# A graph layer on one core: PSUM banks and loads of the lead-in changed, a fourth bank for slot products

## The chip, the cores and the metric

The kernel runs on one core of a Trainium2 chip. The time is device microseconds of one launch. Where one profiled execution is read, its span is the time between the first and the last recorded instruction.

## The reference

A graph of 6250 nodes (128 features each, float32) and 100000 edges, sorted by their destination. Every edge has one of two types, and each type its own weight and bias; each node sums the messages that come to it, adds its own product, and is normalized:

```python
m_data = X[src] @ W_data.T + b_data
m_ctrl = X[src] @ W_control.T + b_control
msg = where((edge_type == 0)[:, None], m_data, m_ctrl)
agg = segment_sum(msg, dst, num_segments=6250)
out = relu(agg + (X @ W_self.T + b_self))
x = layernorm(x + out)          # over the 128 features
```

## The kernel before

**Products.** The messages are made per node, not per edge: 6250 x 2 types. In the lead-in, 25 steps (`q`) of two blocks of 128 nodes each form `x @ [W_data, W_control]` in a PSUM bank of 512 columns (the bias matmul is L499, the two products L502). The result is kept as three bf16 parts in `m3`: ScalarE copies the bank (part 1, L507), TensorE subtracts that part in the bank through a matmul with minus the identity (L510), a copy by ScalarE or VectorE takes part 2 (`evict`, L444 or L445), and VectorE subtracts part 2 from the bank into part 3 (L514). Every second step the parts go to a DRAM `table` (L518). The `x` pieces come by SyncE's queue (L479): the first ones at once, each later one once the copy of part 1 seven steps before it is done.

**Sums.** The destinations are cut into 39 windows of 160 nodes. A window's sum is a product of a selection matrix with the messages in `m3`. It goes in 25 slot products: stage 1 (L956, four matmuls of 384 columns) gathers source rows for 128 slots into a PSUM bank `g`; ScalarE or VectorE copies it to `gs` (L444, L445); stage 2 (L970, four matmuls of 384 columns, and L973, three of 128) adds the slots to their destinations in an accumulating bank `a`. One slot product is therefore eleven matmuls of 8 x 384 + 3 x 128 = 3456 columns. A closing part adds the nodes' own products (L527, L530, L561) and normalizes.

**Ranks.** What a slot gathers is worked out on the chip, for groups of windows (of 1, 2, and nine times 4; the groups begin at windows 0, 1, 3, 7, 11, 15, 19, 23, 27, 31 and 35). The edges of a group are turned into one-hot rows `hots` (four pieces, one buffer each). Counts (TensorE, L713) go through `csb` to DRAM as `past` (SyncE, L720) and come back into the last four rows of `hots` (SyncE, L724, four loads). Then 22 rank rounds (L738 on TensorE, L744 on VectorE, one PSUM bank `rk`) find each edge's slot; a scatter (L775) places them in `vt`; a copy `vs` goes to DRAM as `packed` (SyncE, L795). From `packed`, each window loads `rows`, 784 KB broadcast over the partitions (SyncE, L927, a ring of three buffers, so that a window's load waits for stage 1 of the window three before it), and VectorE makes the selection from them (L935).

**The order** on every engine is fixed by a planner when the kernel is built. Each operation is added with its engine, a duration from a formula (`act(cols)`, `dve(cols)` or a constant) and a due time; buffers are rings of a given number. The planner simulates these and writes the instructions in the order that comes out. On the chip, each engine runs its row in that order, and SyncE issues its loads and stores in that order too. So a changed duration or number of buffers changes the order everywhere.

**PSUM** has eight banks: `vt` 1, `rk` 1, `ga` 1, `a` 2, `g` 3. Bank `ga` serves group 0's ranks and, much later, the "gathered part" (L1050, L1057), which does the last ten nodes (6250 - 39 x 160) through an indirect load.

Of the kernel before, what the change touches and what calls it, by code (L numbers as in the profile page):

```python
# [10 lines left out]
F32 = mybir.dt.float32  # L11
# [6 lines left out]
ACT = mybir.EngineType.Activation  # L18
# [3 lines left out]
P = 128  # L22
D = 128
# [21 lines left out]
NW = sum(GROUPS)  # L45
# [3 lines left out]
NS = 25  # L49
# [5 lines left out]
GT = [slots_of(16 * min(GN, N - NW * WN - GN * i)) for i in range(NGB)]  # L55
# [187 lines left out]
def dve(cols, rate=1.04):  # L243
    return 0.07 + cols * rate / 1000


def act(cols):
    return 0.055 + cols / 1200

def sums_over_windows(ctx, tc, x, xt, edges, w, bias, out, total):  # L250
    nc = tc.nc
    V, A, G, T, S = nc.vector, nc.scalar, nc.gpsimd, nc.tensor, nc.sync
# [19 lines left out]
    T0 = 36.0  # L272
    TW = 13.0
    LAT = 0.1
    G0, G1 = 0.0, -4
    GC = 1.3
    SPD = 0.45
    RP, RA, RS = 1, 14, 0.9
# [5 lines left out]
        lat=4.0)  # L284
    w_sb = C([D, D3], F32, "w_sb")
# [72 lines left out]
    minus = C([P, P], BF16, "minus")  # L358
# [4 lines left out]
    one3 = C([P, P], BF16, "one3")  # L363
# [17 lines left out]
    def count_rows():  # L381
        for h in range(RH):
# [28 lines left out]
                                    start=True, stop=True), 0.8, [first_f, ident], [first_ps])  # L411
# [22 lines left out]
    brows = C([P, D3], BF16, "brows")  # L434
# [18 lines left out]
    m3 = C([P, NT, D3], BF16, "m3")  # L453
# [3 lines left out]
    past_b = Buf(plan, None, None, None, "past_b")  # L457
    m3_key = lambda g: [(m3, (min(g, NS - 1), i)) for i in range(3)]
    MS = 1.3
    LATE = [12.0, 14.0, 20.0]  # L460
    XB = [12, 12, 12, 13]
    xts = []
# [10 lines left out]
                pieces[q0 + k - i] = (c, k, (xts[c], i))  # L473
            loads[q0 // 2] = (c, i, j, q0)

    def load_x(q, after):
        if q in loads:
            c, i, j, q0 = loads[q]
            add("SP", SPD, lambda: S.dma_start(  # L479
                xf(c)[:, i * P : j * P], xt[:, q0 * P : (q0 + j - i) * P]),  # L480
                4.0 + MS * q - 9, after, [(xts[c], i)], lat=3.0)
    AHEAD = 7
    for q in range(AHEAD):
        load_x(q, [])
    for q in range(NS):
        bs = range(2 * q, min(2 * q + 2, NB))
        nb = len(bs)
        due = 4.0 + MS * q
        mp = B(ps, [P, 512], F32, *(("a", 2) if q % 5 > 2 else ("g", 3)))

        n = 2 * nb * D
        ts = slice(4 * q, 4 * q + 2 * nb)

        for i, b in enumerate(bs):
            c, k, xk = pieces[b]

            def product(i=i, c=c, k=k, mp=mp, nb=nb):
                if i == 0:
                    T.matmul(mp.t[:, : 2 * nb * D].rearrange("p (b f) -> p b f", b=nb), one3.t,  # L499
                             brows.t[:, None, : 2 * D].to_broadcast([P, nb, 2 * D]), start=True,  # L500
                             stop=False, skip_group_check=True)
                T.matmul(mp.t[:, 256 * i : 256 * i + 256], xf(c)[:, k * P : k * P + P],  # L502
                         w_sb.t[:, : 2 * D], start=False, stop=False, skip_group_check=True)
            add("PE", 0.5 if i else 0.71, product, due + 0.5 * i, [xk, w_sb, one3, brows], [mp])
        pv3 = lambda mp=mp, nb=nb: mp.t[:, : 2 * nb * D].rearrange("p (t f) -> p t f", f=D)
        mv3 = lambda i, ts=ts: m3.t[:, ts, i * D : (i + 1) * D]
        add("ACT", act(n), lambda pv3=pv3, mv3=mv3: A.copy(mv3(0), pv3()), due + 0.6, [mp],  # L507
            [(m3, (q, 0))])
        load_x(q + AHEAD, [(m3, (q, 0))])
        add("PE", 0.11 * nb, lambda mp=mp, mv3=mv3, nb=nb: T.matmul(  # L510
            mp.t[:, : 2 * nb * D], minus.t, mv3(0), start=False, stop=True,
            skip_group_check=True), due + 1.2, [minus, (m3, (q, 0))], [mp])
        evict(lambda mv3=mv3: mv3(1), pv3, n, due + 1.8, [mp], [(m3, (q, 1))])
        add("DVE", dve(n), lambda pv3=pv3, mv3=mv3: V.tensor_sub(mv3(2), pv3(), mv3(1)),  # L514
            due + 2.4, [mp, (m3, (q, 1))], [(m3, (q, 2))])
# [114 lines left out]
    def ranks(gi, w0, nw, when, step, engines):  # L630
# [6 lines left out]
        n = nw * KT  # L637
# [43 lines left out]
        else:  # L681
# [235 lines left out]
    def sums(gi, w0, nw, placed):  # L917
# [5 lines left out]
        for i in range(nw):  # L923
# [68 lines left out]
    def gathered(bis, when, step):  # L992
# [37 lines left out]
        for j, bi in enumerate(bis):  # L1030
# [51 lines left out]
    for gi, w0, nw, *_ in todo:  # L1082
# [167 lines left out]
```

## Time and profile before

| | |
|---|---|
| runs | 641.18, 645.41, 647.32 us (median 645.41) |
| the profiled execution | 644.74 us, its span 642.9 us |
| granted TensorE clock, mean | 0.967 |
| TensorE busy | 555.6 us, 86% of the span |
| VectorE busy | 496.3 us, 77% |
| ScalarE busy | 487.6 us, 76% |
| GpSimd busy | 31.3 us, 5% |
| copies `gs` on ScalarE | 927, 391.8 us in sum |
| chain that ended last | TensorE 68%, ScalarE 12%, VectorE 7%, DMA 5% |

Windows are named by their number; 975 slot products (39 x 25) make most of the time. A row of a timeline gives the start, the length, the engine, the line and the tiles of a run of equal instructions, and in brackets how long the engine stood idle before it and what ended that. Line numbers here are those of the kernel before; the changed kernel's are 5 to 11 higher.

### The profile page before, as it was taken

Reading aid. Unit: us, or ns where it says so; the run is one execution under the profiler, and the core shown is the slowest. Engines: PE = TensorE matmul, PEld = TensorE weight load, DVE = VectorE, ACT = ScalarE, POOL = GpSimd, SP = SyncE. Lnnn points to the kernel's source line nnn. Section 1 sums busy time; section 2 is a strip of 40 time slices with the busy share of each in tenths; the row PEclk is TensorE's granted clock in tenths of the full one; section 3 lists DMA queues with packets and bytes.
Section 4 is the critical chain, followed back from the end, with each engine's and each line's share of the span. In section 5 each row is a group of like instructions: output and inputs, shape, how many; then the busy total and the mean of one; then the engine's idle time right before and its main releaser. Section 6 shows DMA issues by size and latency. Waiting matters only on the chain.

```text
span 642.9 us, 32170 instructions
## 1 busy us (share of the span) xinstructions
PE 555.6 (86%) x13810; PEld 427.6 (67%) x13810; DVE 496.3 (77%) x1502; ACT 487.6 (76%) x1258; POOL 31.3 (5%) x32
## 2 busy tenths in 40 slices
PE   5878789459989989898998899889889988989992
PEld 3544567338868777776787687678768767766771
DVE  6679688948988898788699979879987988685411
ACT  3545678348879787787888788888889788778992
POOL 1000100100010001001000100100010010010000
PEclk9989899759999999999999999999999999999997
DMA  3895821162045105403520630351253054022300
GB/s 109 244 303 160 246 58 50 22 188 80 3 125 153 44 33 181 107 6 125 135 63 29 188 106 4 125 165 32 73 147 94 5 185 104 17 90 95 82 16 15
DMA packets 56060, 64.33 MB, mean 100 GB/s; under 512 B 18159, under 2 KB 47828, under 8 KB 55908
## 3 DMA queue, kind: packets, MB, share of 16 engines
q1 hardware_dynamic: 54417, 59.68, 31.0%
q0 software_dynamic: 1120, 2.23, 1.6%
q8 instruction: 110, 1.80, 1.2%
q14 instruction: 43, 0.34, 0.2%
q10 hardware_dynamic: 370, 0.26, 0.2%
HBM read 45.94 MB, written 14.30 MB: 94 GB/s over the span
## 4 chain that ended last, share of the span: by engine, by line
PE 68%; ACT 12%; DVE 7%; DMA 5%; issue 5%; SPq 1%; another core or an unknown queue 0%; ACTq 0%; POOLq 0%; DVEq 0%
PE a L970 24%; PE g L956 23%; ACT gs L444 7%; PE rk L738 5%; PE a L973 5%; PE vt L775 3%; ACT to_d L451 3%; DMA hots<-past 2%; PE rk L713 1%; DVE slot L744 1%; PE g L502 1%; PE a L527 1%; DMA rows<-packed 1%; DVE rows L935 1%; PE vt L862 1%
## 5 line engine op out<-in xcount | busy, mean ns | idle before, releaser
L444 ACT CAST gs<-g 128x384 bf16<-128x384 f32 x927 | 391.8, 483 | 85.4 <-PE g L956 69.1
L956 PE MATMUL g<-m,rows 128*32 128x384 bf16 x3822 | 364.1, 331 | 14.0 <-DVE rows L935 8.4
L970 PE MATMUL a<-gs,hot 128*32 128x384 bf16 x3744 | 341.8, 333 | 34.1 <-ACT gs L444 21.0
L956 PEld LDWEIGHTS <-rows 128*32 128x32 bf16 x3822 | 250.4, 134 | 26.5 <-DVE rows L935 9.5
L970 PEld LDWEIGHTS <-hot 128*32 128x32 bf16 x3900 | 172.7, 95 | 103.7 <-issue 61.9
L973 PE MATMUL a<-gs,hot 128*32 128x128 bf16 x2808 | 231.9, 220 | 0.3 <-issue 0.3
L744 DVE TENSOR_REDUCE slot<-rk 124x4 f32<-124x392 f32 x209 | 117.4, 562 | 49.3 <-PE rk L738 42.8
L973 PEld LDWEIGHTS <-hot 128*32 128x32 bf16 x2925 | 116.7, 97 | 8.4 <-issue 4.6
L943 DVE TENSOR_TENSOR hot<-iota_b,to_d 128x1280 bf16<-128x1280 bf16 (+1 forms) x117 | 95.7, 841 | 0.0
L738 PE MATMUL rk<-hots,tri 128*32 128x392 bf16 (+1 forms) x880 | 86.1, 324 | 9.5 <-DMA hots<-past 5.3
L702 DVE TENSOR_TENSOR hots<-iota_b,st 124x784 bf16<-124x784 bf16 (+2 forms) x120 | 58.6, 506 | 4.9 <-PE vt L775 4.9
L935 DVE TENSOR_SCALAR rows<-rows,pid 128x1568 bf16<-128x1568 bf16 x78 | 46.9, 622 | 16.2 <-DMA rows<-packed 16.1
L738 PEld LDWEIGHTS <-tri 128*32 128x32 bf16 x968 | 38.4, 96 | 18.6 <-issue 13.5
L884 POOL DMA_INDIRECT sr<-table,at x20 | 25.9, 1293 | 476.4 <-DVE to_d L877 425.6
L570 DVE TENSOR_REDUCE s<-a 128x128 f32<-128x384 f32 x39 | 21.7, 556 | 34.6 <-PE a L973 22.9
L775 PEld LDWEIGHTS <-two 124*64 124x64 bf16 x858 | 21.7, 110 | 12.2 <-DVE two L766 5.9
L775 PE MATMUL vt<-hots,two 124*64 124x98 bf16 x836 | 26.1, 210 | 3.4 <-DVE two L766 1.7
L451 ACT COPY to_d<-vs 32x100 bf16<-32x100 bf16 (+3 forms) x84 | 22.2, 265 | 1.3
L760 DVE TENSOR_TENSOR hr<-slot_f,slot 124x768 bf16<-124x768 bf16 (+2 forms) x39 | 20.2, 517 | 2.6 <-ACT slot L448 2.6
L444 ACT CAST gl<-g 64x384 bf16<-64x384 f32 x39 | 18.4, 472 | 4.7 <-PE g L956 4.7
L713 PE MATMUL rk<-hots,later 124*32 124x392 bf16 (+1 forms) x210 | 20.8, 335 | 0.8 <-DVE slot L744 0.8
L766 DVE TENSOR_TENSOR two<-hr,lo 124x768 bf16<-124x768 bf16 (+2 forms) x39 | 20.2, 517 | 0.1
(188 smaller groups left out, 502.1 us busy)
## 6 DMA issues: line engine op xcount, KB each, us to landing
rows<-packed SPq DMA_DIRECT2D x39, 784.0 KB
table<-m SPq DMA_DIRECT2D x12, 768.0 KB
xc<-in_xt SPq DMA_DIRECT2D x9, 320.0 KB
rows<-in_xt SPq DMA_DIRECT2D x8, 256.0 KB
xr<-in_x SPq DMA_DIRECT2D x8, 256.0 KB
out<-xr SPq DMA_DIRECT2D x8, 256.0 KB
gl<-sr SPq DMA_DIRECT2D x39, 48.0 KB
win<-in_edges SPq DMA_DIRECT2D x38, 32.0 KB
```

Source lines behind the costliest of these rows:

```text
L444: [("ACT", act(cols), lambda: A.copy(o(), src())), ("DVE", dve(cols), lambda: V.tensor_copy(o(), src()))], None, None, due, r, w, lat)
L451: "ACT", 0.1 + cols / 1000, lambda: A.copy(o(), src()), due, r, w)
L702: lambda k=k, kn=kn, ci=ci, hs4=hs4: V.tensor_tensor(hv(ci)[:EP, k - KS[ci] : k - KS[ci] + kn].rearrange("p k w (c d) -> p (k w) c d", d=2 ...
L713: T.matmul(cnt.t[R * j : R * j + R, :wide], later.t[:EP, R - 1 - k : 2 * R - 1 - k], flat(k, EP), start=k < 4, stop=k + 4 > KT - 2, skip_g ...
L738: T.matmul(acc.t[R * j : R * j + R, (k - k0) * wide : (k - k0 + 1) * wide], tri.t[:, R * j : R * j + R], flat(k, P), start=k == k0, stop=True,
L744: vec(due, (k1 - k0) * wide, lambda k0=k0, k1=k1, acc=acc: V.tensor_reduce(slot.t[:, k0:k1, :], acc.t[:EP, : (k1 - k0) * wide].rearrange(" ...
L775: T.matmul(vv()[q : q + 64, i // 2, :], two.t[:EP, (k - k0) * nw + i].rearrange("p f r -> p (f r)"), one(k)[:EP, i, :], start=k == 0 and i ...
L935: add("DVE", dve(half * NT, 0.335), lambda sp=sp, rs=rs: V.tensor_scalar(sp.t[:, rs], sp.t[:, rs], pid1.t, None, op0=ALU.is_equal), due - ...
L943: lambda i=i, hot2=hot2, s4=s4, c0=c0, c1=c1: V.tensor_tensor(hot2.t[:, c0:c1].rearrange("p g (c d) -> p g c d", d=2), iota1_b.t.rearrange ...
L956: T.matmul(gp.t[R * t : R * t + R, :D3], sp.t[:, :, 4 * g + t], m3.t[:, 4 * g + t, :], start=True, stop=True)
L970: T.matmul(a.t[R * j : R * j + R, :D3], hot2.t[:, g, R * j : R * j + R], gs.t, start=g == 0, stop=False, skip_group_check=True)
L973: T.matmul(a.t[R * c : R * c + R, D3:], hot2.t[:, g, P:], gs.t[:, c * D : (c + 1) * D], start=False, stop=last, skip_group_check=True)
```

## The change

- `act(cols)`, the planner's duration for a ScalarE copy, is 0.12 + 0.00085 per column instead of 0.055 + 1/1200; the durations of the lead-in's matmuls are lower too.
- The ring of `g` has four banks instead of three, and the bank `ga` is gone: group 0's ranks share `rk` with the others, and the gathered part uses an `a` bank, at the time of window 20.
- The lead-in's message products use the four `g` and two `a` banks (six); before, three `g` and two `a`.
- All `x` pieces are asked for at the start; before, the later ones waited for a part 1 each.
- Part 2 is always copied by ScalarE. In even steps, part 3 is made by a second minus-identity matmul and a copy, by ScalarE or VectorE, instead of VectorE's subtraction.

The diff, with what only renames left out:

```diff
 def act(cols):
-    return 0.055 + cols / 1200
+    return 0.12 + cols * 0.00085
...
-    G0, G1 = 0.0, -4
+    G0 = 20
...
     MS = 1.3
+    LOP = 2
...
-    def load_x(q, after):
+    def load_x(q):
...
-                4.0 + MS * q - 9, after, [(xts[c], i)], lat=3.0)
-    AHEAD = 7
-    for q in range(AHEAD):
-        load_x(q, [])
+                -9.0 + 0.5 * q, [], [(xts[c], i)], lat=3.0 + 0.6 * q)
+    for q in range(NS):
+        load_x(q)
...
-        mp = B(ps, [P, 512], F32, *(("a", 2) if q % 5 > 2 else ("g", 3)))
+        if q % 6 < 4:
+            mp, half = B(ps, [P, 512], F32, "g", 4), 0
+        else:
+            mp, half = B(ps, [P, 512], F32, "a", 2), 0
...
-            add("PE", 0.5 if i else 0.71, product, due + 0.5 * i, [xk, w_sb, one3, brows], [mp])
+            add("PE", 0.43 if i else 0.64, product, due + 0.5 * i, [xk, w_sb, one3, brows], [key])
...
-        load_x(q + AHEAD, [(m3, (q, 0))])
...
-        evict(lambda mv3=mv3: mv3(1), pv3, n, due + 1.8, [mp], [(m3, (q, 1))])
-        add("DVE", dve(n), lambda pv3=pv3, mv3=mv3: V.tensor_sub(mv3(2), pv3(), mv3(1)),
-            due + 2.4, [mp, (m3, (q, 1))], [(m3, (q, 2))])
+        add("ACT", act(n), lambda pv3=pv3, mv3=mv3: A.copy(mv3(1), pv3()), due + 1.8, [key],
+            [(m3, (q, 1))])
+        if q % LOP:
+            add("DVE", dve(n), lambda pv3=pv3, mv3=mv3: V.tensor_sub(mv3(2), pv3(), mv3(1)),
+                due + 2.4, [key, (m3, (q, 1))], [(m3, (q, 2))])
+        else:
+            add("PE", 0.11 * nb, lambda f=less_part: f(1), due + 2.4, [minus, (m3, (q, 1))], [key])
+            evict(lambda mv3=mv3: mv3(2), pv3, n, due + 3, [key], [(m3, (q, 2))])
...
-        bank = "rk" if gi else "ga"
+        bank = "rk"
...
-                gp = B(ps, [P, 512], F32, "g", 3)
+                gp = B(ps, [P, 512], F32, "g", 4)
...
-            ga = B(ps, [P, 512], F32, "ga", 1)
+            ga = B(ps, [P, 512], F32, "a", 2)
...
-    g0, g1 = T0 + G0, T0 + (NW + G1) * TW
-    step = max((g1 - g0) / max(sum(GT), 20), GC + 0.02)
+    g0, step = T0 + G0 * TW, GC + 0.02
```

**SyncE at the start of the program.** The `rows` and `hot2` tiles here hold pieces of `x` (they lend their buffers), `win` is the edges of a group, `table` the parts on their way to DRAM. Before:

```order
L428 DMA win_94<-in_edges 124x66
L479 DMA rows_106<-in_xt 128x256 x2
L479 DMA rows_106<-in_xt 128x512 x2
L479 DMA rows_136<-in_xt 128x512
L920 DMA xc_192<-in_xt 128x160
L479 DMA rows_136<-in_xt 128x512
L518 DMA table_72<-m3_212 128x8x384
```

Now:

```order
L480 DMA rows_94<-in_xt 128x256 x2
L480 DMA rows_94<-in_xt 128x512 x2
L480 DMA rows_127<-in_xt 128x512
L428 DMA win_136<-in_edges 124x66
L480 DMA rows_127<-in_xt 128x512 x2
L480 DMA rows_155<-in_xt 128x512 x3
L480 DMA hot2_171<-in_xt 128x512 x2
L480 DMA hot2_171<-in_xt 128x640
```

The first edges stand behind five pieces of `x` instead of ahead of all of them, and the later pieces stand ahead of the first `table`.

**SyncE where the group of windows 11 to 14 begins.** `packed` holds the slots of this group, `rows` are its windows' selections, `past` and `hots` are the next group's counts on their way out and back. Before:

```order
L795 DMA packed_73<-vs_6317 128x2x98
L927 DMA rows_6495<-packed_73 128x3136
L927 DMA rows_6515<-packed_73 128x3136
L720 DMA past_74<-csb_6541 128x392
L724 DMA hots0_5486<-past_74 4x2352
L927 DMA rows_6667<-packed_73 128x3136
```

Now:

```order
L806 DMA packed_73<-vs_6403 128x2x98
L731 DMA past_74<-csb_6502 128x392
L938 DMA rows_6598<-packed_73 128x3136
L938 DMA rows_6609<-packed_73 128x3136
L938 DMA rows_6624<-packed_73 128x3136
L735 DMA hots0_5548<-past_74 4x2352
```

`past` has moved ahead of the first two selections, and the third selection ahead of `hots`.

**TensorE at the same place.** `g` and `a` are the banks of stage 1 and stage 2, `rk` the bank of a rank round; `rows_6495` belongs to window 11. The rows of before around the first rank round of the next group, without those that repeat:

```order
L970 MATMUL a_6699<-gs_6741,hot2_6497 32x384
L973 MATMUL a_6699<-gs_6741,hot2_6497 32x128
L956 LDWEIGHTS rows_6495
L956 MATMUL g_6774<-m3_212,rows_6495 32x384
L956 MATMUL g_6779<-m3_212,rows_6495 32x384
L738 LDWEIGHTS tri_185
L738 MATMUL rk_6786<-hots0_5486,tri_185 32x392
```

Now, where `hot2_5696` belongs to window 10, `vt_6665` is the closing part of windows 7 to 10, and `rows_6598` belongs to window 11:

```order
L981 MATMUL a_6137<-gl_4983,hot2_5696 32x384
L984 MATMUL a_6137<-gl_4983,hot2_5696 32x128
L572 MATMUL vt_6665<-bs_6658,fold_146 32x128
L538 MATMUL vt_6665<-w_sb_77,xb_2799 32x128 x4
L541 MATMUL vt_6665<-brows_83,one3_87 32x128
L749 MATMUL rk_6684<-hots0_5548,tri_151 32x392
L967 LDWEIGHTS rows_6598
L967 MATMUL g_6692<-m3_210,rows_6598 32x384
```

Before, the first rank round stands in the middle of window 11's products, seven products after its first. Now it stands ahead of the first of them, right behind the closing part. Between the last scatter (L775, now L786) and that round TensorE has 94 stage 1 matmuls, 88 of L970 and 66 of L973 before, and 38, 56 and 42 now. The round stands ahead of the new group's first product in the same way at windows 15, 19, 27 and 31, and also at window 3; not at 7, 23 and 35.

More of the change, by code (lines that the diff above doesn't have):

```diff
@@ L488, in sums_over_windows @@
         due = 4.0 + MS * q
-        mp = B(ps, [P, 512], F32, *(("a", 2) if q % 5 > 2 else ("g", 3)))
+        if q % 6 < 4:
+            mp, half = B(ps, [P, 512], F32, "g", 4), 0
+        else:
+            mp, half = B(ps, [P, 512], F32, "a", 2), 0
+        key = (mp, half)
+        mt = lambda mp=mp, half=half: mp.t[:, half] if len(mp.shape) == 3 else mp.t
         n = 2 * nb * D
@@ L503, in product, with less_part @@
                          w_sb.t[:, : 2 * D], start=False, stop=False, skip_group_check=True)
-            add("PE", 0.5 if i else 0.71, product, due + 0.5 * i, [xk, w_sb, one3, brows], [mp])
-        pv3 = lambda mp=mp, nb=nb: mp.t[:, : 2 * nb * D].rearrange("p (t f) -> p t f", f=D)
+            add("PE", 0.43 if i else 0.64, product, due + 0.5 * i, [xk, w_sb, one3, brows], [key])
+        pv3 = lambda mt=mt, nb=nb: mt()[:, : 2 * nb * D].rearrange("p (t f) -> p t f", f=D)
         mv3 = lambda i, ts=ts: m3.t[:, ts, i * D : (i + 1) * D]
-        add("ACT", act(n), lambda pv3=pv3, mv3=mv3: A.copy(mv3(0), pv3()), due + 0.6, [mp],
+        def less_part(i, mt=mt, mv3=mv3, nb=nb):
+            T.matmul(mt()[:, : 2 * nb * D], minus.t, mv3(i), start=False, stop=True,
+                     skip_group_check=True)
@@ L508, in sums_over_windows @@
+        add("ACT", act(n), lambda pv3=pv3, mv3=mv3: A.copy(mv3(0), pv3()), due + 0.6, [key],
             [(m3, (q, 0))])
-        load_x(q + AHEAD, [(m3, (q, 0))])
-        add("PE", 0.11 * nb, lambda mp=mp, mv3=mv3, nb=nb: T.matmul(
-            mp.t[:, : 2 * nb * D], minus.t, mv3(0), start=False, stop=True,
-            skip_group_check=True), due + 1.2, [minus, (m3, (q, 0))], [mp])
-        evict(lambda mv3=mv3: mv3(1), pv3, n, due + 1.8, [mp], [(m3, (q, 1))])
-        add("DVE", dve(n), lambda pv3=pv3, mv3=mv3: V.tensor_sub(mv3(2), pv3(), mv3(1)),
-            due + 2.4, [mp, (m3, (q, 1))], [(m3, (q, 2))])
+        add("PE", 0.11 * nb, lambda f=less_part: f(0), due + 1.2, [minus, (m3, (q, 0))], [key])
```

6 lines of the change are left out of this document (3 added, 3 removed).

## The prediction

> **What bounds the kernel now.** I read the page's sums first. Each row gives an engine's busy time, its share of the span, and its instructions.
>
> ```profile
> span 642.9 us, 32170 instructions
> PE 555.6 (86%) x13810; PEld 427.6 (67%) x13810; DVE 496.3 (77%) x1502; ACT 487.6 (76%) x1258; POOL 31.3 (5%) x32
> PE 68%; ACT 12%; DVE 7%; DMA 5%; issue 5%; SPq 1%; another core or an unknown queue 0%; ACTq 0%; POOLq 0%; DVEq 0%
> ```
>
> TensorE is busy for 86% of the span and makes 68% of the chain that ended last (third line). Time is to be won where TensorE stands idle, and lost where it stands idle longer. I then split the span by stages. A row is a stretch, its length, busy times with counts, the granted clock, the DMA share and GB/s.
>
> ```profile
> core 0: us, PE busy (x) PEld busy (x) DVE busy (x) ACT busy (x) POOL busy (x), PEclk, DMA share, GB/s
> 40.80:44.20 3.40, 0.00 (x0) 0.02 (x1) 1.29 (x5) 1.01 (x3) 0.00 (x0) 0.96 0.88 279
> 44.20:47.60 3.40, 3.39 (x22) 1.73 (x21) 2.04 (x4) 0.75 (x2) 0.00 (x0) 0.54 0.83 251
> 120.93:137.01 16.08, 3.94 (x59) 2.31 (x60) 9.28 (x37) 4.81 (x15) 3.72 (x2) 0.50 0.61 174
> 236.38:251.50 15.12, 11.93 (x317) 9.14 (x321) 12.88 (x51) 11.61 (x32) 2.56 (x2) 1.00 0.52 179
> 251.50:292.80 41.30, 38.60 (x1055) 31.49 (x1045) 34.63 (x85) 34.39 (x90) 0.00 (x0) 1.00 0.25 60
> 596.15:607.07 10.92, 10.48 (x292) 8.10 (x287) 4.50 (x9) 10.26 (x27) 0.00 (x0) 1.00 0.41 115
> ```
>
> The fifth and sixth rows are one group of four windows, from its scatter (236.38) to the next group's first rank round (251.50), and from there to the next scatter: 56.42 us. TensorE is idle for 15.12 - 11.93 = 3.19 us of the first, the boundary, and for 41.30 - 38.60 = 2.70 us of the second. The fourth row is the same piece of the program ahead of window 3: TensorE does 3.94 us of work in 16.08, at half the clock. So one boundary of this kernel is covered by products and another is a hole. The timelines show why. First the covered one:
>
> ```profile
> 235.75 0.63 PE L775 MATMUL vt<-hots,two 124*64 124x98 bf16 x20
> 236.76 0.38 SPq L795 DMA_DIRECT2D packed<-vs  x1
> 238.59 0.83 SPq L927 DMA_DIRECT2D rows<-packed  x2
> 242.79 0.34 PE L713 MATMUL rk<-hots,later 124*32 124x392 bf16 x3
> 245.14 0.50 ACT L444 CAST csb<-rk 128x392 bf16<-128x392 f32 x1
> 245.34 2.23 DVE L935 TENSOR_SCALAR rows<-rows,pid 128x1568 bf16<-128x1568 bf16 x4
> 245.67 0.32 SPq L720 DMA_DIRECT2D past<-csb  x1
> 247.76 0.27 SPq L724 DMA_DIRECT2D hots<-past  x1
> ```
>
> Then the hole:
>
> ```profile
> 121.31 0.39 SPq L795 DMA_DIRECT2D packed<-vs  x1
> 125.41 0.33 SPq L720 DMA_DIRECT2D past<-csb  x1
> 125.83 1.34 SPq L927 DMA_DIRECT2D rows<-packed  x3
> 127.32 1.92 SPq L724 DMA_DIRECT2D hots<-past  x4
> 133.99 1.18 PE L956 MATMUL g<-m,rows 128*32 128x384 bf16 x12 [7.97 <-DVE rows L935]
> 137.01 0.52 PE L738 MATMUL rk<-hots,tri 128*32 128x392 bf16 x4 [1.84 <-DMA hots<-past]
> ```
>
> In the first, `hots` follows two selections, and TensorE has two dozen products to do meanwhile. In the hole `past`, three selections and `hots` go in a row, and the rank round starts 137.01 - 125.83 = 11.2 us after the selections are issued.
>
> **The change, part by part.**
>
> *The boundaries.* By the order, SyncE's row at window 11 now reads as it does in the hole: `packed`, `past`, three `rows`, `hots`. On TensorE the first rank round stands ahead of window 11's first product, so nothing of the new group can pass it. The same holds at windows 15, 19, 27 and 31: five boundaries. The planner believes that `hots` is there by then; the chip decides.
>
> The work that covers the boundary: from scatter to rank round the order has 94 stage 1 matmuls, 88 of L970 and 66 of L973 before, and 38, 56 and 42 now. In columns that is (56 + 32) x 384 + 24 x 128 = 36864, or 10.7 products of 3456 columns. One product's time is the step between neighbours where nothing waits:
>
> ```profile
> 259.39 0.44 PE L970 MATMUL a<-gs,hot 128*32 128x384 bf16 x4
> 259.78 0.44 PE L970 MATMUL a<-gs,hot 128*32 128x384 bf16 x4
> ```
>
> That is 0.39 us, so 4.2 us of work leave the boundary (11.93 becomes 7.7) and are done later (38.60 becomes 42.8).
>
> When `hots` lands: the last counts now stand about five and a half products behind the scatter (2.1 us), their copy and the issue of `past` take some 1 us more, so the selections go out 3.1 us behind the scatter; with the hole's 11.2 us the rank round starts at 14.3. Upper end: in the hole the selections went out at 125.83 - 120.92 = 4.9, which gives 16.1. Lower end, from the rate:
>
> ```profile
> GB/s 0 0 27 0 0 0 84 0 0 10 418 335 324 387 408 439 335 156 51 82 94 151 9 0 59 157 199 408 366 185 179 198 190 120 100 72 39 77 79 97
> rows<-packed SPq DMA_DIRECT2D x3, 784.0 KB
> ```
>
> The first row has the rates from 234 to 258 us in slices of 0.6. The two selections issued at 238.59 move from 240.0 on, at a mean of 378 GB/s over seven slices. Three of 784 KB are 2.41 MB, 6.4 us. Issued 2.2 us after the scatter as now (238.59 - 236.38), 1.4 us until they move, 6.4 us, and some 1.5 us for `hots` behind them: 11.5. I take 14.3, since the hole is this very sequence.
>
> Then TensorE is idle for 14.3 - 7.7 = 6.6 us in one piece. After the 3.40 us without a matmul in the second row of the windows, the next 3.40 us ran at a granted 0.54 (third row); I charge half of 3.4, less a little: 1.6 us. The Trainium skill ("TensorE: Matmul & The Clock Gate", section "HAM oscillation — how this bites in real kernels") tells of the same fall behind waits of over 3.4 us, with 1.67 us throttled behind each, of which half is lost; by it the term would be 0.8, and the sum 4 us less. The row has a longer stretch of low clock than that, so it decides.
>
> *The fourth bank.* With three banks TensorE's waits in the steady part (185.8 to 520 us) are these: for what, sum, times, longest.
>
> ```profile
> PE a L970 <- ACT gs L444: 11.7, 23, 1.5
> PE a L970 <- DVE gs L445: 3.4, 6, 0.8
> PE g L956 <- ACT gs L444: 2.9, 3, 1.0
> ```
>
> 18.0 us in 334 is all that it can reach. By the order, stage 1 stood two products ahead of stage 2 for 805 of the 975, and stands three ahead for 697 now; I take half of the 2.70 us idle in a group's second part, 1.35 (between 0 and 2.70). In the last four windows ScalarE is busy for 10.26 of 10.92 us (last window row): the planner gives 22 more of the copies to VectorE there and elsewhere, -1.0 (0 to -2).
>
> So a group with a changed boundary takes 14.3 + 42.8 + 1.35 + 1.6 = 60.05 us instead of 56.42: +3.63, five times, **+18.2**. Three other boundaries (7, 23, 35) keep their cover: 3 x -1.35 = **-4.05**. The last windows: **-1.0**.
>
> *The lead-in.* Its rows: a stall on `hots`, the loads ahead of it, the shape that is thinned out, the copies, and a stretch in which VectorE is full.
>
> ```profile
> 31.30 1.20 SPq L479 DMA_DIRECT2D hot<-in_xt  x1
> 39.01 2.80 SPq L724 DMA_DIRECT2D hots<-past  x3
> 44.21 0.52 PE L738 MATMUL rk<-hots,tri 128*32 128x196 bf16 x8 [3.42 <-DMA hots<-past]
> L514 DVE TENSOR_TENSOR m<-g,m 128x512 bf16<-128x512 f32 x15 | 10.3, 685 | 4.3 <-ACT m L444 4.3
> L507 ACT CAST m<-g 128x512 bf16<-128x512 f32 x15 | 8.9, 590 | 9.2 <-PE g L502 7.8 <-PE ga L713 1.4
> L510 PE MATMUL g<-m,minus 128*128 128x512 bf16 x15 | 6.1, 415 | 0.0
> 60.00:70.00 10.00, 7.93 (x171) 5.72 (x175) 10.00 (x22) 4.69 (x13) 0.00 (x0) 0.83 0.54 165
> ```
>
> 13 subtractions leave VectorE (685 ns each, 8.9 us); it is full only near the end (10.00 of 10), so I count some five at 0.6: -3.0 (0 to -8). In exchange come 13 matmuls (0.415 each, 5.4 us on TensorE) and 14 copies (0.59 each, 8.3 us on ScalarE). TensorE has 2 us free in those ten and ScalarE 5.3, which hides them; uncovered, TensorE's would cost 5.4. The stall of 3.42 us comes while late `x` pieces (31.30 and on) and `past` share the queue; with `x` asked for at the start it goes, with its half clock (1.56): -5.0 (0 to -5). One rank bank for groups 0 and 1 puts group 0's rounds behind group 1's counts: +1.5 (0 to +3). The first edges stand behind five `x` pieces, +1.0 (0 to +3.8, what five pieces, 1.05 MB, take at the 279 GB/s of the second window row). At window 3 a rank round now stands ahead of the first product, which started 3 us earlier than it; part of that was covered: +1.2. The gathered part's move costs nothing: two slots in a bank that is free for most of a window; at worst one wait, 1 us. Sum of the lead-in: **-4.3**.
>
> Together: +18.2 - 4.05 - 1.0 - 4.3 = +8.8. The profiled execution took 644.74 us, 0.7 below the median of the runs, so it stands for them: **653.6 us**. With the ends of the landing (11.5 and 16.1, five times -2.8 and +1.8: -14 and +9) and of the lead-in, its own range is 640 to 668.
>
> **The rivals.**
>
> *Faster: the boundaries cost nothing.* If `hots` doesn't queue behind the three selections but lands within the 7.7 + 3.19 us that the boundary has now, only the gains are left: 8 x -1.35 - 1.0 - 4.3 = -16.1, **628.6 us**. For it: the waits of 18.0 us show that there is something to win. Against it: the hole. Chance 0.22.
>
> *The boundaries cost about what the gains give.* With the landing at its lower end a group takes 11.5 + 42.8 + 1.35 + 1.6 = 57.25, five times +0.83 = +4.2, less 9.35: **639.6 us**. For it: no cover was there in the hole, here SyncE and ScalarE run on. Chance 0.24.
>
> *Slower: the fourth bank gives nothing.* Stage 1 ahead by three instead of two helps only where a copy is late by a bank's time; if the waits of L970 are ScalarE's own lateness, they stay. Then the sum is higher by 8 x 1.35 + 1.0 = 11.8: **665.4 us**. It decides where the share of ScalarE's copies is what limits. The Trainium skill (same page and section) reports a kernel in which "Adding PSUM double-buffering gave no further gain (125.5 µs)" once its loop kept TensorE fed; 18.0 us of 334 is near that state. Chance 0.12.
>
> That the change doesn't do what it says is excluded: the order shows the lead of stage 1 and the banks.
>
> **How the numbers follow.** The forecast has 0.42. About 1% (6.4 us, so 639 to 652) is what a measurement of this kernel can tell from no change. Of the forecast's 0.42 a third, 0.13, lies below 652. Of the second rival's 0.24 a third, 0.08, lies below 639. So faster is 0.22 + 0.08 = 0.30, same 0.16 + 0.13 = 0.29, slower 0.29 + 0.12 = 0.41. The range leaves out most of the first rival (0.15) and the top: 633 to 667. Cases of both signs hold mass; the likeliest one's own range is 640 to 668.
>
> **What would show it.** At window 11 of the new trace: the rank round (now L749) ahead of window 11's first stage 1, released by the DMA of `hots`, about 14 us behind the scatter, with an idle time of 5 to 8 us and a granted clock near half behind it; the same at 15, 19, 27 and 31, and not at 23. If that idle time is under 3 us, the first rival is right. The waits for `gs` in the steady part should fall from 18.0 us to about half; if they don't, the third rival is. In the lead-in the stall of 3.42 us at the first rank rounds should be gone, and VectorE no longer full from 60 to 70 us. A period outside the five groups that differs from 56.4 - 1.35 by over 2 us would make the sum wrong whatever the boundaries do.

## The result, and the profile after

The changed kernel takes 665.63 us (median of 4 runs, 662.07 to 666.55), the kernel before 643.91 beside it: a ratio of **1.0324**, with a 95% interval of 1.0257 to 1.0392. It is slower, as forecast, but by 3.2% where the forecast had 1.4% (653.6 us). The profiled execution has a span of 665.0 us, 22.1 more than before's.

The sums of the changed kernel's page, and its waits of TensorE from 185.8 to 520 us (what waited for what, sum, times, longest):

```profile
span 665.0 us, 32167 instructions
PE 560.1 (84%) x13823; PEld 443.8 (67%) x13823; DVE 503.5 (76%) x1530; ACT 473.3 (71%) x1230; POOL 29.8 (4%) x32
```

```profile
PE rk L749 <- DMA hots<-past: 24.0, 5, 6.0
PE a L981 <- ACT gs L444: 8.6, 21, 2.2
PE g L967 <- ACT gs L444: 2.9, 4, 0.9
```

Of the three waits for `gs` of before (18.0 us) two are left, 11.5 us, and a new one stands above them: the rank rounds wait for `hots`. The timeline of the changed kernel where window 11 begins shows how it comes about.

```profile
231.73 0.63 PE L786 MATMUL vt<-hots,two 124*64 124x98 bf16 x20
232.75 0.38 SPq L806 DMA_DIRECT2D packed<-vs  x1
234.12 0.67 PE L724 MATMUL rk<-hots,later 124*32 124x392 bf16 x8
234.65 0.94 DVE L854 TENSOR_TENSOR hl<-iota_b,pos 124x1536 bf16<-124x1536 bf16 x1
235.59 0.55 DVE L445 CAST csb<-rk 128x392 bf16<-128x392 f32 x1
236.17 0.35 SPq L731 DMA_DIRECT2D past<-csb  x1
236.62 3.67 SPq L938 DMA_DIRECT2D rows<-packed  x3
240.39 1.34 SPq L735 DMA_DIRECT2D hots<-past  x4
248.03 0.52 PE L749 MATMUL rk<-hots,tri 128*32 128x392 bf16 x4 [5.76 <-DMA hots<-past]
```

This is the hole's sequence. The counts end at 234.79, but their copy `csb` stands behind `hl` in VectorE's row and starts at 235.59; before, ScalarE made it. So the selections go out 4.3 us behind the scatter's end (232.36). They keep SyncE for 3.67 us, since the third needs its buffer back (SyncE waits 2.4 us there for a stage 1); `hots` is issued 8.0 us behind the scatter's end, and its data are used 7.6 us after that. In the boundary of before the round came 3.7 us after that issue (247.76 to 251.50), without a wait. The other four boundaries that the prediction named have the same wait, and so has window 3 (first row):

```profile
134.33 0.52 PE L749 MATMUL rk<-hots,tri 128*32 128x392 bf16 x4 [11.70 <-DMA hots<-past]
309.84 0.52 PE L749 MATMUL rk<-hots,tri 128*32 128x392 bf16 x4 [5.87 <-DMA hots<-past]
370.27 0.52 PE L749 MATMUL rk<-hots,tri 128*32 128x392 bf16 x4 [5.98 <-DMA hots<-past]
489.66 0.52 PE L749 MATMUL rk<-hots,tri 128*32 128x392 bf16 x4 [5.37 <-DMA hots<-past]
550.94 0.52 PE L749 MATMUL rk<-hots,tri 128*32 128x392 bf16 x4 [5.69 <-DMA hots<-past]
```

By stretches, in the columns of before's windows: the boundary at 11, the 4 us behind it, the whole group from scatter to scatter, then window 23's boundary and rest.

```profile
232.36:248.03 15.67, 8.30 (x205) 5.79 (x206) 12.75 (x48) 6.93 (x21) 2.50 (x2) 0.91 0.69 194
248.03:252.03 4.00, 4.00 (x58) 3.06 (x61) 1.30 (x2) 2.59 (x6) 0.00 (x0) 0.50 0.39 84
232.36:294.04 61.68, 52.67 (x1389) 42.71 (x1393) 49.70 (x147) 44.63 (x118) 2.50 (x2) 0.94 0.32 84
414.93:432.90 17.97, 15.55 (x398) 11.45 (x401) 15.75 (x59) 13.83 (x40) 2.49 (x2) 1.00 0.56 185
432.90:474.19 41.29, 38.70 (x1045) 32.67 (x1036) 33.27 (x90) 32.24 (x84) 0.00 (x0) 0.96 0.18 46
```

The next table takes the end of each group's last scatter (start plus length of its row, as 231.73 + 0.63) as a mark, and gives the time from mark to mark; each stretch begins with the boundary named.

| stretch | before, us | after, us | difference |
|---|---|---|---|
| start to the mark ahead of window 3 | 120.92 | 117.56 | -3.4 |
| boundary 3 | 59.52 | 59.26 | -0.3 |
| boundary 7 | 55.93 | 55.54 | -0.4 |
| boundaries 11, 15, 19, 27, 31 (sum of five) | 279.10 | 303.04 | +23.9 |
| boundary 23 | 55.81 | 59.26 | +3.4 |
| boundary 35 to the end | 71.62 | 70.34 | -1.3 |
| sum | 642.90 | 665.00 | +22.1 |

The loss is in the five boundaries whose order had changed; window 23's stretch is longer too.

### The profile page after: what moved, and what is told of

Its sections match the earlier page's. It is cut to its first block, busy times and chain, and to the rows that moved or that the text cites. A ratio compares the mean times of both kernels' runs of the same rounds, so it can differ in the third digit from the quotient of the medians.

```text
span 665.0 us, 32167 instructions
## 1 busy us (share of the span) xinstructions
PE 560.1 (84%) x13823; PEld 443.8 (67%) x13823; DVE 503.5 (76%) x1530; ACT 473.3 (71%) x1230; POOL 29.8 (4%) x32
## 4 chain that ended last, share of the span: by engine, by line
PE 67%; DMA 15%; ACT 7%; DVE 6%; issue 2%; SPq 1%; another core or an unknown queue 1%; ACTq 0%; DVEq 0%
PE g L967 26%; PE a L981 21%; DMA hots<-past 8%; PE rk L749 6%; PE a L984 4%; DMA rows<-packed 3%; PE vt L786 3%; ACT gs L444 3%; ACT to_d L451 2%; PE g L507 2%; DMA past<-csb 1%; DVE slot L755 1%; DVE hots L713 1%; DVE s L581 1%; PE a L538 1%
## 5 line engine op out<-in xcount | busy, mean ns | idle before, releaser
L444 ACT CAST gs<-g 128x384 bf16<-128x384 f32 x905 | 373.4, 498 | 122.5 <-PE g L967 115.3
L981 PE MATMUL a<-gs,hot 128*32 128x384 bf16 x3744 | 372.4, 335 | 19.5 <-ACT gs L444 16.6
L967 PE MATMUL g<-m,rows 128*32 128x384 bf16 x3822 | 376.9, 340 | 9.7 <-ACT gs L444 4.3
L984 PE MATMUL a<-gs,hot 128*32 128x128 bf16 x2808 | 240.9, 222 | 0.0
L981 PEld LDWEIGHTS <-hot 128*32 128x32 bf16 x3900 | 176.9, 97 | 61.9 <-issue 36.4
L755 DVE TENSOR_REDUCE slot<-rk 124x4 f32<-124x392 f32 (+2 forms) x214 | 120.0, 561 | 53.7 <-PE rk L749 37.3
L749 PE MATMUL rk<-hots,tri 128*32 128x392 bf16 (+1 forms) x880 | 104.3, 334 | 45.6 <-DMA hots<-past 42.0
L984 PEld LDWEIGHTS <-hot 128*32 128x32 bf16 x2925 | 124.7, 98 | 8.0 <-issue 0.2
L581 DVE TENSOR_REDUCE s<-a 128x128 f32<-128x384 f32 (+1 forms) x40 | 22.2, 555 | 32.1 <-PE g L967 18.1
L786 PEld LDWEIGHTS <-two 124*64 124x64 bf16 x858 | 22.4, 113 | 14.9 <-DVE two L777 11.0
L445 DVE CAST gs<-g 128x384 bf16<-128x384 f32 x31 | 17.1, 551 | 20.0 <-PE g L967 12.9
L786 PE MATMUL vt<-hots,two 124*64 124x98 bf16 x836 | 26.8, 214 | 4.8 <-DVE two L777 4.6
L444 ACT COPY bs<-a 96x128 f32<-96x128 f32 x39 | 10.2, 261 | 19.4 <-DVE s L581 13.2
```

The source lines that it names most:

```text
L444: [("ACT", act(cols), lambda: A.copy(o(), src())), ("DVE", dve(cols), lambda: V.tensor_copy(o(), src()))], None, None, due, r, w, lat)
L581: vec(da, D3 + 70, lambda a=a, s=s, m=m: V.tensor_reduce(s.t[:m], a.t[:m, :D3].rearrange("p (c d) -> p d c", c=3), axis=AX.X, op=ALU.add), ...
L749: T.matmul(acc.t[R * j : R * j + R, (k - k0) * wide : (k - k0 + 1) * wide], tri.t[:, R * j : R * j + R], flat(k, P), start=k == k0, stop=True,
L755: vec(due, (k1 - k0) * wide, lambda k0=k0, k1=k1, acc=acc: V.tensor_reduce(slot.t[:, k0:k1, :], acc.t[:EP, : (k1 - k0) * wide].rearrange(" ...
L786: T.matmul(vv()[q : q + 64, i // 2, :], two.t[:EP, (k - k0) * nw + i].rearrange("p f r -> p (f r)"), one(k)[:EP, i, :], start=k == 0 and i ...
L967: T.matmul(gp.t[R * t : R * t + R, :D3], sp.t[:, :, 4 * g + t], m3.t[:, 4 * g + t, :], start=True, stop=True)
```

## The experiments

The theory: the five boundaries lost their cover, because the plan's order of `past`, selections, `hots` and the first rank round had moved, while the fourth bank and the lead-in are worth something by themselves. The rival: the new parts cost by themselves, through the copies that went to VectorE and through slower matmuls. "Cover" below is the number of slot products that the order has between the scatter and the next rank round. All ratios are to the kernel before, beside it on the same chip.

**1. The changed kernel, ranks due earlier.** One number of the plan moves.

```diff
-            when, step, engines = T0 + w0 * TW - 58, 1.0, ["SP"]
+            when, step, engines = T0 + w0 * TW - 62, 1.0, ["SP"]
```

> The changed kernel, with the due times of the groups' ranks 4 us earlier (58 becomes 62); by the order every boundary then has 23 to 30 products between the scatter and the next rank round, as before the change, and the round stands inside the new window. Theory (the five uncovered boundaries made the loss): about 636 us, with no wait for the hots load over 2 us from window 7 on. Rival (the copies moved to VectorE and the slower matmuls inside the groups made it): 655 us or more, with the waits for hots gone all the same.

Measured: 622.35 us, ratio **0.9744** (0.9692 to 0.9796), faster than both kernels and than the 636 us expected. The same boundary, and the same group with its 1389 matmuls:

```profile
223.43 0.63 PE L786 MATMUL vt<-hots,two 124*64 124x98 bf16 x20
226.65 0.83 SPq L938 DMA_DIRECT2D rows<-packed  x2
231.29 0.32 SPq L731 DMA_DIRECT2D past<-csb  x1
235.27 1.28 SPq L735 DMA_DIRECT2D hots<-past  x4
236.59 0.34 SPq L938 DMA_DIRECT2D rows<-packed  x1
237.59 0.35 PE L749 MATMUL rk<-hots,tri 128*32 128x392 bf16 x4 [0.83 <-DMA hots<-past]
```

```profile
224.07:237.59 13.52, 11.06 (x301) 9.08 (x301) 11.30 (x42) 12.06 (x33) 1.90 (x2) 1.00 0.43 156
224.07:277.83 53.76, 49.75 (x1389) 43.01 (x1393) 47.96 (x140) 44.66 (x120) 1.90 (x2) 1.00 0.32 97
```

The rank round still starts 13.5 us behind the scatter, only 2.2 earlier. But TensorE has 301 matmuls to do meanwhile where it had 205, and the group takes 53.76 us for 61.68. The rival falls: all the new parts are still in. That not every wait is gone shows at 293.60 (2.64 us for `hots`); the expectation had at most 2.

**2. The changed kernel with the old cost of a copy.**

```diff
-    return 0.12 + cols * 0.00085
+    return 0.055 + cols / 1200
```

> The changed kernel with the old planner cost of a ScalarE copy; everything else stays, the fourth bank too. By the order each boundary has 17 to 18 products and the rank round stands inside the new window. Theory (order at the boundaries): 640 to 648 us, idle times at the boundaries of 2 to 4 us. Rival (the banks or the lead-in made the loss): 655 us or more.

Measured: 651.23 us, **1.0183** (1.0144 to 1.0223): slower than expected. The rank round stands inside the new window here, and now the window's first product waits, for its selection, 3.7 to 5.0 us at the boundaries from window 7 on. The one at window 11:

```profile
247.90 1.51 PE L967 MATMUL g<-m,rows 128*32 128x384 bf16 x16 [4.56 <-DVE rows L946]
```

So neither the rank round's place ahead of the window nor the new cost is needed for a loss. The first thing that needs a load of the new group waits, and 17 to 18 products are too few to cover it.

**3. The new lead-in alone**, on three banks, with the old cost and bank `ga`.

```diff
-        if q % 6 < 4:
-            mp, half = B(ps, [P, 512], F32, "g", 4), 0
+        if q % 5 < 3:
+            mp, half = B(ps, [P, 512], F32, "g", 3), 0
...
-        bank = "rk"
+        bank = "rk" if gi else "ga"
...
-                gp = B(ps, [P, 512], F32, "g", 4)
+                gp = B(ps, [P, 512], F32, "g", 3)
```

> The new lead-in alone (all x asked for at once, half of the third parts by TensorE, part 2 by ScalarE) with three banks for slot products, the old planner cost and group 0's own rank bank; boundaries as in the kernel before by the order. Theory: the lead-in is worth -3 to -5 us, so 639 to 641. Rival (the lead-in costs): 650 or more.

Measured: 636.46 us beside 638.25, **0.9972** (0.9943 to 1.0001). The lead-in doesn't cost; it is worth about 1.8 us here, less than expected, and its interval touches none.

**4. The banks and the new cost alone**, with the old lead-in.

```diff
 def act(cols):
-    return 0.055 + cols / 1200
+    return 0.12 + cols * 0.00085
...
-        bank = "rk" if gi else "ga"
+        bank = "rk"
...
-                gp = B(ps, [P, 512], F32, "g", 3)
+                gp = B(ps, [P, 512], F32, "g", 4)
```

> The old lead-in with the four banks, the new planner cost and the gathered part at window 20: by the order the boundaries are those of the changed kernel (12 products at five of them). Theory: the loss is all here, 665 to 672 us. Rival (the lead-in costs): 650 or less.

Measured: 666.80 us, **1.0435** (1.0405 to 1.0465). The loss is all here, and 1.1% more than with the new lead-in.

The runs so far also tell which edits moved the order. Between the third and the second experiment only the banks differ: the cover falls from 20 to 23 products (counted in the third's trace) to 17 or 18, and the ratio rises from 0.997 to 1.018. Between the second and the changed kernel only the cost differs: from there to 12 products, and 1.032.

**5. The second kernel with cover.** Old cost, four banks, ranks due 8 us earlier.

```diff
-    return 0.12 + cols * 0.00085
+    return 0.055 + cols / 1200
...
-            when, step, engines = T0 + w0 * TW - 58, 1.0, ["SP"]
+            when, step, engines = T0 + w0 * TW - 66, 1.0, ["SP"]
```

> Four banks and the new lead-in with the old planner cost of a copy (as the second experiment), and the ranks' due times 8 us earlier (66 for 58): by the order 28 products cover each boundary instead of 17 to 18. Theory (what counts is how many products lie between the scatter and the first thing that needs the new loads): 622 to 632 us, no wait over 2 us at the boundaries from window 7 on. Rival (the old cost is itself bad with four banks): 645 us or more.

Measured: 622.85 us, **0.9678** (0.9611 to 0.9745). With 28 products instead of 17 to 18 the same cost and the same banks go from 1.8% slower to 3.2% faster.

**6. The first kernel with three banks.**

```diff
-                gp = B(ps, [P, 512], F32, "g", 4)
+                gp = B(ps, [P, 512], F32, "g", 3)
...
-            when, step, engines = T0 + w0 * TW - 58, 1.0, ["SP"]
+            when, step, engines = T0 + w0 * TW - 62, 1.0, ["SP"]
```

The message products go back to three `g` banks, group 0 to bank `ga`, as in the third.

> The first experiment's kernel (ranks 4 us earlier, new planner cost, new lead-in) with three banks for slot products and group 0's own rank bank; 25 products cover each boundary. Theory (the fourth bank gives half of the idle time inside a group, 1.35 us a group): 632 to 638 us. Rival (the bank gives nothing, the first experiment's gain came from the order alone): 622 to 625 us.

Measured: 639.54 us, **0.9939** (0.9905 to 0.9973), just above the range expected for the theory. The fourth bank is worth 0.9939 - 0.9744, about 2% or 12.5 us, where the boundaries are covered; without it, earlier ranks change little. The difference holds the lead-in's banks too (six or five), and covers of 23 and 25 products.

**7. The selections on GpSimd's queue**, else the changed kernel.

```diff
-                add("SP", SPD, lambda i=i, sp=sp, j=j: S.dma_start(
+                add("POOL", SPD, lambda i=i, sp=sp, j=j: G.dma_start(
```

> The changed kernel with the selections' loads issued by GpSimd on its own queue; TensorE's order at the boundaries stays (12 products, rank round ahead of the new window), SyncE's row is packed, past, hots with no selection between. If the hots load is late because it stands behind three selections in SyncE's queue, the wait for hots shrinks to under 2 us at the boundaries of windows 11, 15, 19, 27 and 31 and the new window's products wait for their selection instead, about 3 to 5 us. If it is late because the memory system is full of the selections' bytes, or because past is late, the wait for hots stays at 5 to 6 us. Time 655 to 670 us by either.

Measured: 645.03 us, **1.0030** (0.9992 to 1.0068), better than either expectation, and between the two on the waits. At window 11 `hots` leaves SyncE 1.8 us behind `past` and the wait shrinks to 2.38; at window 27 it leaves 7.6 us behind, and the wait stays (5.69).

```profile
234.25 0.35 SPq L731 DMA_DIRECT2D past<-csb  x1
236.08 1.50 SPq L735 DMA_DIRECT2D hots<-past  x4
241.68 0.35 PE L749 MATMUL rk<-hots,tri 128*32 128x392 bf16 x4 [2.38 <-DMA hots<-past]
462.35 0.35 SPq L731 DMA_DIRECT2D past<-csb  x1
469.91 1.66 SPq L735 DMA_DIRECT2D hots<-past  x4
473.16 0.52 PE L749 MATMUL rk<-hots,tri 128*32 128x392 bf16 x4 [5.69 <-DMA hots<-past]
```

With no selection in SyncE's row, `hots` still took 5.6 us from issue to use at window 11 (7.6 in the changed kernel). So the queue is one part of the lateness. Why `hots` was issued so late at window 27, with nothing between it and `past`, the list of SyncE's waits shows: it waited for `past` to land.

```profile
SPq L735 <- DMA past<-csb: 7.1, 1, 7.1
```

At window 11 that wait is 1.4 us. GpSimd issued the first two selections there 0.4 us behind `past`, at window 27 1.1 us ahead of it (461.30). The other three boundaries agree: `hots` is issued 1.8 us behind `past` at 15, where the selections go out behind `past`, and 4.9 us behind at 19 and 31, where they go out ahead of it. So at these five boundaries a small transfer issued behind selections landed late although they were on another queue. What the two queues share isn't shown.

**8. The planner told that `hots` lands late.**

```diff
-                [(hots[ci], ("c", ci))], lat=2.0)
+                [(hots[ci], ("c", ci))], lat=7.0)
```

> The changed kernel with one number of the plan put right: the planner is told that a hots load takes 7 us to land instead of 2. By the order 22 to 39 products then cover each boundary. Theory: 622 to 635 us. Rival (cover isn't what counts): 655 us or more.

Measured: 648.86 us, **1.0063** (1.0021 to 1.0104): 2.6% better than the changed kernel's ratio, but above what was expected. Its mark ahead of window 3 stands at 131.31 us, for 117.56 in the changed kernel: the same number moves the first groups' ranks too, where there is no cover to be had. The profiled execution is the longest of its runs (653.41 us; the others take 642.93 to 650.62), so these 13.8 us are an indication. They aren't all: behind that mark the run takes 520.5 us, and the first experiment takes 504.9 behind its own, for the same 12273 matmuls, though no wait for `hots` over 0.5 us is left. What makes that difference stays open, so a long cover alone doesn't give the first experiment's time.

**9. TensorE kept busy through the wait.**

```diff
             def rank(k0=k0, k1=k1, acc=acc):
+                for _ in range(30 if gi in (5, 6, 7, 9, 10) and k0 == 0 else 0):
+                    T.matmul(acc.t[:, :wide], minus.t,
+                             m3.t[:, :2, :].rearrange("p t f -> p (t f)")[:, :wide],
+                             start=True, stop=True, skip_group_check=True)
```

> The changed kernel in its order, with 30 matmuls of 392 columns (about 4.9 us) into the rank bank, whose result is not used, ahead of the first rank round at the five boundaries of windows 11, 15, 19, 27 and 31, inside the wait for hots. If half the clock behind the wait is a part of the loss, they keep TensorE busy, the granted clock stays at 1 behind the wait, and the kernel gets about 5 x 2.9 = 14.6 us faster than the changed one (2.9 us is the difference in TensorE's busy time for the same 1389 matmuls of a group between the changed kernel and the first experiment): 648 to 653 us. If the clock costs what the prediction took, 1.6 each: 658. If it costs nothing or the matmuls delay the round: 665 us or more.

Measured: 656.78 us, **1.0303** (1.0220 to 1.0386), not told apart from the changed kernel's 1.0324; the run was too noisy for the question. The profile has the mechanism: the 4 us behind the rank round at windows 11, 19 and 27.

```profile
251.40:255.40 4.00, 4.00 (x66) 3.03 (x68) 1.30 (x2) 2.85 (x7) 0.00 (x0) 0.57 0.30 72
372.28:376.28 4.00, 3.86 (x103) 3.14 (x106) 1.86 (x3) 3.36 (x9) 0.00 (x0) 1.00 0.29 70
490.22:494.22 4.00, 3.86 (x103) 3.15 (x106) 1.86 (x3) 3.36 (x9) 0.00 (x0) 1.00 0.40 87
```

At 19, 27 and 31, where 1.5 to 1.7 us of waiting were left, the granted clock stayed at 1.00 and the 4 us held 103 matmuls instead of 58. At 11 and 15, where 2.5 us were left, it fell to 0.57 and 0.64. The 30 matmuls took 5.15 us each time. So 45 matmuls, at 4 us for 103, are 1.7 us a boundary: the prediction's 1.6, and not the 2.9 expected here, which had put all the difference in busy time down to the clock.

**10. The fifth kernel with the selections on GpSimd's queue.**

```diff
-                add("SP", SPD, lambda i=i, sp=sp, j=j: S.dma_start(
+                add("POOL", SPD, lambda i=i, sp=sp, j=j: G.dma_start(
```

> The fifth experiment's kernel (four banks, new lead-in, old planner cost, ranks 8 us earlier, 28 products of cover) with the selections' loads on GpSimd's queue. Where the cover is long enough already, taking the selections out of SyncE's queue is worth nothing at the boundaries from window 7 on; only the hole ahead of window 3 (7.1 and 2.7 us of waits) can shrink: 616 to 623 us. If the queue still costs at every boundary: under 612.

Measured: 619.95 us, **0.9678** (0.9560 to 0.9795), the fifth's ratio. Where the cover is long enough, the queue is worth nothing that this measurement can tell.

**11. Five products of cover.** The second kernel, with later rank rounds.

```diff
-    return 0.12 + cols * 0.00085
+    return 0.055 + cols / 1200
...
-    LATE = [12.0, 14.0, 20.0]
+    LATE = [12.0, 14.0, 23.0]
```

> The second experiment's kernel (four banks, new lead-in, old planner cost) with the ranks' rounds due 3 us later (23 for 20): by the order only 5 products cover the boundary at six places (17 at window 23), and the rank round stands just inside the new window. Theory (cover counts): 12 products fewer than the second experiment are 4.7 us of idle time more at six places, and the clock behind it, so 651 + 28 + up to 9 = 675 to 690 us. Rival (17 products were already too few to matter, or the old cost alone makes the loss): 645 to 655 us.

Measured: 699.08 us, **1.0991** (1.0907 to 1.1074): beyond the upper end. A boundary now waits twice, for the selection and then for `hots`:

```profile
256.14 1.50 PE L967 MATMUL g<-m,rows 128*32 128x384 bf16 x16 [5.64 <-DVE rows L946]
262.28 0.52 PE L749 MATMUL rk<-hots,tri 128*32 128x392 bf16 x4 [4.63 <-DMA hots<-past]
```

The fifth, second and eleventh differ only in when the ranks are due: a cover of 28, 17 to 18 and 5 products gives 0.968, 1.018 and 1.099.

**12. The first kernel with the old lead-in.** The fourth kernel, with the edit of the first:

```diff
-            when, step, engines = T0 + w0 * TW - 58, 1.0, ["SP"]
+            when, step, engines = T0 + w0 * TW - 62, 1.0, ["SP"]
```

> The first experiment's kernel with the old lead-in (x pieces one behind another, third parts all by VectorE): four banks, new planner cost, the gathered part at window 20, ranks 4 us earlier, 23 products of cover. What the new lead-in is worth where the boundaries are covered: by the third experiment (0.3% of the kernel before) this one's ratio to the kernel before is 0.977, 2 us above the first experiment; by the difference between the fourth experiment and the changed kernel (1.1%) it is 0.985, 7 us above. If the lead-in costs: 0.972 or less.

Measured: 630.67 us, **0.9889** (0.9855 to 0.9924), 1.4% above the first experiment. The second case of the expectation holds, and a little more. Two rows show what the old lead-in has in this version, with group 0's rounds in the bank of the others:

```profile
39.65 0.60 PE L738 MATMUL rk<-xr,tri 128*32 128x98 bf16 x20 [3.75 <-DVE slot L744]
64.72 0.52 PE L738 MATMUL rk<-hots,tri 128*32 128x196 bf16 x8 [6.11 <-DVE slot L744]
```

In the first experiment no wait of TensorE between 10 and 70 us is over 1 us. So the lead-in's worth, 0.3% on the old banks and 1.1 to 1.4% on the new, hangs on the banks: it seems to make up for the one that group 0 gave away. Which of its three edits does so wasn't tried.

## Why the prediction was right or wrong

**Right.** *The place.* Five boundaries named from the order have the new wait, released by `hots`, in the idle time foreseen (5.4 to 6.0 us for 5 to 8). At windows 7 and 23 it stays short (1.0 us at 7). *Half the clock behind the wait*: 0.50 to 0.53 granted in the next 4 us of the five, worth 1.7 us by the ninth experiment; the term was 1.6. The Trainium skill's figure ("TensorE: Matmul & The Clock Gate", section "HAM oscillation — how this bites in real kernels"), a loss of half of 1.67 us, is too small here. *The fourth bank's worth*: 11.8 us as priced in the third rival, about 12.5 by the sixth experiment; the price was half of an idle time, taken by choice, so that it comes so near is in part luck. The third rival fell: its 665.4 us stand beside the measured 665.63 by luck, since the bank does give something and the boundaries cost more. The sentence of the same section of the Trainium skill, that more PSUM buffering gave nothing further, doesn't carry over: here TensorE does wait for the copies out of PSUM (18.0 us of the 334 before, 11.5 after). The faster rival's number, 628.6 us for covered boundaries, was of the right kind: 622 to 623 came when the order was mended; it was wrong only for this kernel's order.

**Wrong: the size.** The sum had +8.8, the profiles have +22.1. Four points make up the account.

1. *The marks move.* The step "a group with a changed boundary takes ..." compared times from scatter to scatter as if each held the same work. The scatters of the changed kernel stand elsewhere among the products: counted from the columns of the matmuls in the two traces, the five stretches hold 485 products for 497 before, and the stretches of 7, 23 and 35 hold 11 more (4.4, 3.4 and 3.0). At 0.39 us a product, the five look 12 x 0.39 = 4.7 us better than they are, and the three others 4.2 worse. At equal work the five cost 23.9 + 4.7 = +28.6, and the three others give 1.8 - 4.2 = -2.4 (1.8 from -0.4 + 3.4 - 1.3).
2. *The five boundaries*: +18.2 in the sum, so 10.4 too little. The landing has most of it: 14.3 us behind the scatter was taken, 15.5 to 16.2 measured, 15.8 on average, five times 1.5 = 7.5. The step made it from 3.1 us until the selections go out and the hole's 11.2 from there. The second part held: 11.3 to 12.1 us at the five, though SyncE is held for 3.67 us by the third selection, which it wasn't in the hole (1.34). The first part failed: 4.2 us at each of the five, since "their copy and the issue of `past` take some 1 us more" left out that VectorE makes `hl` ahead of that copy. The other error is the base. The step took the group at window 11 for all of them, and its 56.42 us stop at 292.80, 0.49 us ahead of the next scatter's end:

```profile
292.66 0.63 PE L775 MATMUL vt<-hots,two 124*64 124x98 bf16 x20
```

   From mark to mark that group takes 56.91 us, and the five average 279.10 / 5 = 55.82: 1.09 a group, 5.4 in all. Against these 12.9 us the rest of the group, clock and all, was charged about 0.5 us a group too high once the 0.49 us are put back, 2.5 in all.
3. *"Three other boundaries keep their cover", -4.05, and the last windows, -1.0*: -5.05 in the sum, -2.4 at equal work. The kept cover was right. By stretch the three give -2.1 (window 7), +2.1 (23) and -2.4 (35), so the whole shortfall is in window 23's stretch, the one that breaks the prediction's last sign (59.3 us for 56.4 - 1.35, over 2 us apart). Its boundary has no wait for `hots`. Its rows have another wait, some ten microseconds behind the first rank round: VectorE waits for a group's edges, ScalarE for VectorE, TensorE for ScalarE, and the clock falls behind it (last row, a stretch).

```profile
441.10 0.25 DVE L667 TENSOR_SCALAR cb<-win 124x88 int32<-124x88 int32 x1 [1.91 <-DMA win<-in_edges]
441.81 0.26 ACT L444 COPY bs<-a 96x128 f32<-96x128 f32 x1 [2.55 <-DVE s L581]
442.51 0.35 PE L981 MATMUL a<-gs,hot 128*32 128x384 bf16 x4 [2.25 <-ACT gs L444]
442.51:446.51 4.00, 4.00 (x72) 3.19 (x74) 2.95 (x9) 3.14 (x8) 0.00 (x0) 0.60 0.16 46
```

4. *The lead-in*: -4.3 forecast up to window 7's boundary, -3.7 measured (-3.4 and -0.3). The stall of 3.42 us is gone, as the step had it, but a wait of 4.28 us for VectorE ahead of a scatter (61.16) is new, and the hole ahead of window 3 stayed, with 11.70 us of waiting in one piece. That the sum is about right is in part luck: in the fourth experiment, with the old lead-in on these banks (and on another chip), the mark ahead of window 3 stands at 126.0 us, some 5 later than before, where the sum had +1.5 for the shared rank bank; the new lead-in's own edits then took off some 8, more than the sum had.

The own range of the forecast, 640 to 668 us, held the time, since the landing's upper end was taken from the hole. The point stood too low because the way to the selections' issue was taken at 3.1 us where 4.2 passed, because one group, read half a microsecond short, stood for five, and because half of the gain elsewhere didn't come.

## What to carry to other kernels

Where a planner writes the order, a change to one ring or one assumed duration can move instructions far from the edit. Count in the new order how much independent work lies between a load's cause and its first user, and compare that with the measured landing: here 28, 17 and 5 products in that place gave 0.97, 1.02 and 1.10 of the time, with only the ranks' due times changed. A resource that was added for good reason (a bank worth 2%) can then show as a loss of the same size (0.997 in the third experiment, 1.018 in the second); before dropping it, look for the place where its cover went.

## What the runs showed of the hardware

A wait in which 2.5 us were left behind 5.15 us of matmuls whose result nobody uses was still followed by a lowered clock (0.57 and 0.64), a wait of 1.5 to 1.7 us was not (1.00). Between them the runs fall on both sides: behind a wait of 2.0 us the first experiment has 0.57 (347.34), behind one of 2.38 the seventh has 1.00 (241.68). A small load, `hots` (pieces of 15 to 18 KB), was used 2.3 us after its issue when no selection stood directly ahead of it (first experiment, 235.27 to 237.59), at most 3.7 in the kernel before, and 7.6 behind three selections of 784 KB. With the selections on another queue, `past` (98 KB) kept SyncE waiting 1.4 us when it was issued ahead of them and 7.1 when it was issued behind them.
